# Four PSUM banks in two shared pairs, one run of value products, fp16 projection halves in a macaron block

## The chip, the cores and the metric

The kernel runs on one core of one Trainium2 chip. The metric is the device time of one execution in microseconds (us), as the median of several executions. The profile shown is that of one further execution of the same program.

## The reference, cut to what matters

The input has 8 sequences of 1024 rows of 256 channels. Three residual steps follow each other: half a feed-forward step, an attention step, half a feed-forward step with the same weights. All matrices are fp32.

```python
x = x + 0.5 * ffn(layernorm(x))      # r = sigmoid(xr @ Wr.T); out = r * (relu(xk @ Wk.T)**2 @ Wv.T)
x = x + attn(layernorm(x))
x = x + 0.5 * ffn(layernorm(x))
# attn, 16 heads of 16 channels: 40 fixed offsets o (0..32, 48, 64, 96, 128, 192, 256, 384)
lg[i] = (q . k[n - o_i]) / 4 * (1 + q . scale_embed[i]) + pos_bias[i]     # masked where n < o_i
p = softmax over the 40 offsets
out = (sum_i p[i] * v[n - o_i]) * if_gain;  return (out * sigmoid(x @ gate_w.T + gate_b)) @ out_w.T + out_b
```

## The kernel before, in words

Rows are worked on in 32 chunks of 256 (feed-forward and projections) and 64 tiles of 128 (attention). Five Python generators emit the work: `stage_f1` and `stage_f2` (the two feed-forward steps), `stage_p` (projections), `stage_qk` (scores) and `stage_att` (the rest of attention). They are advanced step by step in an order that the constants `TRACE` set, each step under a priority that `RANK` sets. A scheduler then chooses the order of the instructions on each engine from these priorities and its own durations, so an edit at one place moves instructions at many others. [...]

The projections (`stage_p`, `proj`) split both operands in two parts, `xh`, `xl` and `wa_hi`, `wa_lo`, and add three products (high·high, high·low, low·high). The parts are of type fp32r, a rounded fp32 of four bytes. There are 4 projections of 12 products in each chunk, so 1536 products of 128 rows x 128 columns x 256.

The scores (`scores`, called by `stage_qk`) are products of 32 rows of queries with keys, four of them side by side in the columns of the array: 16 or 32 of them fill one PSUM tile `p`. ScalarE copies it out (line 308). The results go to HBM (`sl_d` for the near offsets, `sf_d` for the far ones) and come back skewed, as `lg` and `ef`.

For each tile, `stage_att` forms the position products `gp` (two halves of 8 products), and VectorE multiplies them into `lg` (lines 405 and 410). GpSimd adds the bias, VectorE takes the maximum and subtracts it, ScalarE takes the exponential. The probabilities of the near offsets go to HBM and come back as `pd` (lines 426 and 428), in one single buffer. TensorE transposes `pd` in two groups of four (`tra`, line 464), ScalarE copies each group out as `ptt` (line 470), and 32 small value products fill `pv`. VectorE normalises (lines 481 to 485), TensorE transposes `acc` (line 490), VectorE gates it into `yt` (line 491), and for each second tile the output projection follows and is added to `x1` (line 505).

PSUM has eight banks, and before the change each holds one tag with one buffer: `psa`, `psb` and `psp` for the chunks, `psq` for scores, `gp`, `pst` for the transposes of `pd`, `pv`, and `psy` for the transposes of `acc` and for the output projection. A tile can be written only when its tag's buffer has been read out:

```python
p = ps.tile([128, 512], F32, name="p", tag="psq")          # scores
gp = ps.tile([128, 64, 8], F32, name="gp")                 # position products
tr = ps.tile([128, 512], F32, name="tra", tag="pst")       # transposes of pd
tr = ps.tile([128, 512], F32, name="tra", tag="psy")       # transposes of acc, output projection
```

Of the kernel before, what the change touches and what calls it, by code (L numbers as in the profile page):

```python
# [7 lines left out]

F32 = mybir.dt.float32
F32R = mybir.dt.float32r  # L10
F16 = mybir.dt.float16
I32 = mybir.dt.int32
AF = mybir.ActivationFunctionType
ALU = mybir.AluOpType
# [11 lines left out]
NL = LW + 1  # L26
# [11 lines left out]
VPAD = 96  # L38
VROW = 2 * 8 * 17
F2A = 28  # L40
TRACE = (0, 3.6, -4.4, -8.1, -10.6)
RANK = (0, 5.1, -4.4, -8.1, -10.6)

# [6 lines left out]
def macaron(ctx: ExitStack, tc: tile.TileContext, x, wffn, watt, wo, cols, rows, pbias, se, mask, out):  # L50
    nc = tc.nc
    pool = lambda name, bufs, **k: ctx.enter_context(tc.tile_pool(name=name, bufs=bufs, **k))
    const = pool("const", 1)
# [7 lines left out]
    mu_r, mu_k, b_q, b_k, b_g, gain, slot = (col[:, 2 * i : 2 * i + 2] for i in range(7))  # L61
    wot = const.tile([128, 2, 256], F32, name="wot")
    row = const.tile([128, 2, 256], F32, name="row")
    bv, bo = row[:, 0], row[:, 1]
    bias = const.tile([128, NO * 16], F32, name="bias")
    msk = const.tile([128, 3, NO], F32, name="msk")
    wa_hi = const.tile([128, 4, 2, 256], F32R, name="wa_hi")
    wa_lo = const.tile([128, 4, 2, 256], F32R, name="wa_lo")
    seb = const.tile([128, 2, NO], F16, name="seb")
    half = const.tile([128, 4], F32, name="half")  # L70
    nc.gpsimd.memset(half, -0.5)
# [10 lines left out]
    pw = pool("pw", 1)  # L82
# [10 lines left out]
    def load_att():  # L93
        with tc.tile_pool(name="setup", bufs=1) as sp:
            wst = sp.tile([128, 4, 2, 256], F32, name="wst")
            nc.sync.dma_start(wst, watt.rearrange("w (c p) d -> p w c d", p=128))
            nc.vector.tensor_scalar(wst[:, 0], wst[:, 0], 0.25, None, ALU.mult)
            nc.vector.tensor_copy(wa_hi, wst)
            nc.vector.tensor_tensor(wa_lo, wst, wa_hi.bitcast(F32), ALU.subtract)
            nc.vector.tensor_scalar(b_q, b_q, 0.25, None, ALU.mult)  # L100
            nc.vector.tensor_scalar(b_g, b_g, 0.5, None, ALU.mult)
            nc.sync.dma_start(row, rows.unsqueeze(0).to_broadcast([128, 2, 256]))
            for t in [t.bitcast(F32) for t in kb] + vw:
                nc.gpsimd.memset(t, 0.0)
            zero = kb[1].bitcast(F32).rearrange("p a b w -> p (a b w)")
            for i in range(2):
                nc.sync.dma_start(v_d[i][0 : VPAD * VROW].rearrange("(p w) -> p w", p=VPAD), zero[:VPAD, :VROW])
            nc.sync.dma_start(sf_d[0:PADF].rearrange("(p w) -> p w", p=16), zero[:16, : PADF // 16])
            for c0, c1, w in ((0, 8, 384), (8, 15, 384), (15, 16, 368)):
                o = PADF + c0 * ROW + ROW - 384  # L110
                nc.sync.dma_start(flat(sf_d, o, (SF_T, 32), (ROW, c1 - c0), (1, w)), zero[:32, : (c1 - c0) * w])
            nc.sync.dma_start(flat(pd_d, NL * 16, (4 * SKEW, 128), (SKEW, 4), (1, SKEW - NL * 16)), zero[:, : 4 * 512])
            nc.sync.dma_start(bias, pbias.to_broadcast([128, NO * 16]))
            nc.sync.dma_start(msk, mask.rearrange("t p u -> p t u"))
            nc.sync.dma_start(wot, wo.rearrange("(c p) d -> p c d", p=128))
            for c in range(2):
                nc.vector.tensor_scalar(wot[:, c], wot[:, c], gain[:, c : c + 1], 0.5, ALU.mult, ALU.mult)
            se_f = sp.tile([128, NO], F32, name="se_f")
            se_h = sp.tile([128, NO], F16, name="se_h")
            for h2 in range(2):  # L120
                nc.sync.dma_start(se_f[64 * h2 : 64 * h2 + 64], se.unsqueeze(1).to_broadcast([16, 4, NO]))
            nc.vector.memset(seb, 0.0)
            nc.vector.tensor_scalar(se_f, se_f, 4.0, None, ALU.mult)
            nc.vector.tensor_copy(se_h, se_f)
            nc.vector.tensor_tensor(se_f, se_f, se_h, ALU.subtract)
            nc.vector.tensor_scalar(se_f, se_f, slot[:, 1:2], None, ALU.mult)
            for h2 in range(2):
                a = slice(64 * h2, 64 * h2 + 64)
                nc.vector.scalar_tensor_tensor(seb[a, h2], se_h[a], slot[a, 0:1], se_f[a], ALU.mult, ALU.add)
# [3 lines left out]
    def mm(o, l, r, start, stop):  # L133
        nc.tensor.matmul(o, l, r, start=start, stop=stop)  # L134
# [98 lines left out]
    def stage_p():  # L233
        for c in range(NCH):
# [4 lines left out]
            gt = gate[c] = pga.tile([128, 2, 256], F32, name="gt")  # L239
            s = "b" if c == 1 else "p"  # L240
            tr = norm_transposed(x1[c], y, nb, 2 * k, s)
            xh = pw.tile([128, 2, 256], F32R, name="xh", tag="xk" + s)
            xl = pw.tile([128, 2, 256], F32R, name="xl", tag="xr" + s)
            nc.scalar.copy(xh, tr)
            nc.vector.tensor_tensor(xl, tr, xh.bitcast(F32), ALU.subtract)

            def proj(w):
                p = ps.tile([128, 2, 256], F32, name="p", tag="ps" + s)
# [21 lines left out]
                        nc.sync.dma_start(flat(qk_d[i % 2][j], o + ro, (2048, 128), (s2, 2), (1, 256)), hl)  # L270
            p = proj(3)
            for g in range(2):
                nc.scalar.activation(gt[:, g], p[:, g], AF.Tanh, bias=b_g[:, g : g + 1], scale=0.5)
            p = ps.tile([128, 512], F32, name="p", tag="ps" + s)
            for k in range(2):
                first = True
# [20 lines left out]
    def stage_qk():  # L297
        def scores(o, g, q4, q, k, keys):

            p = ps.tile([128, 512], F32, name="p", tag="psq")  # L300
            for pr in range(4):
                for s in range(len(q4(0))):
                    for a in range(4):
                        pp = p[32 * a : 32 * a + 32, pr * 128 : pr * 128 + 128].rearrange("n (h j) -> n h j", h=2)
                        w = 64 // len(q4(a))
                        ms = q4(a)[s]
                        mm(pp[:, :, s * w : s * w + w], q[:, pr, ms], k[:, pr, :, keys(ms)], True, True)
            nc.scalar.copy(o[:, :, :, g], p.rearrange("n (q h j) -> n j h q", q=4, h=2))  # L308

        for i in range(2 * B):  # L310
            hf = i % 2
# [57 lines left out]
    def stage_att():  # L369
        for tt in range(B * NT):  # L370
# [25 lines left out]
                v3[:, 2].rearrange("p h w -> p (h w)"), flat(v_d[b % 2], o - 48 * VROW, (VROW, 128), (1, VROW))  # L396
            )
            for h2 in range(2):
                gp = ps.tile([128, 64, 8], F32, name="gp")
                for g in range(2):  # L400
                    for pr in range(4):
                        q = qs[i, g][:, pr, t4 * 128 : t4 * 128 + 128]
                        mm(gp[:, 0:NO, 4 * g + pr], q, seb[:, h2], True, True)
                e = slice(8 * h2, 8 * h2 + 8)
                nc.vector.scalar_tensor_tensor(
                    lg[:, 0:NL, e], gp[:, 0:NL], 1.0, lg[:, 0:NL, e], ALU.add, ALU.mult
                )
                for k0, k1 in FARG:
                    w0, w1 = (24 - FAR[k] // 16 for k in (k0, k1 - 1))
                    nc.vector.scalar_tensor_tensor(  # L410
                        lf[:, k0:k1, e],
                        gp[:, NL + k0 : NL + k1],
                        1.0,
                        ef[:, w0 : w1 + 1 : (w1 - w0) // (k1 - k0 - 1), e],
                        ALU.add,
                        ALU.mult,
                    )
# [39 lines left out]
                nc.vector.tensor_tensor(o, terms[:, 0:m], terms[:, n - m : n], ALU.add)  # L457
                n -= m

            pv = ps.tile([128, 2, 8, 17], F32, name="pv")  # L460
            for g in range(2):
                tr = ps.tile([128, 512], F32, name="tra", tag="pst")
                for pr in range(4):
                    nc.tensor.transpose(  # L464
                        tr[:, pr * 128 : pr * 128 + 128],
                        pd.rearrange("p (m e) -> p m e", e=8)[:, :, 4 * g + pr],
                        ident,
                    )
                ptt = pw.tile([128, 4, 128], F32, name="ptt")
                nc.scalar.copy(ptt.rearrange("p q n -> p (q n)"), tr)  # L470
                for pr in range(4):
                    for q in range(4):
                        mm(
                            pv[32 * q : 32 * q + 32, :, 4 * g + pr],
                            ptt[:, pr, q:128:4],
                            vwt[:, q, :, 4 * g + pr],
                            True,
                            True,
                        )
            rc = pstat.tile([128, 16], F32, name="rc")  # L480
            nc.vector.tensor_tensor(rc, pv[:, :, :, 16:17].rearrange("p a b o -> p (a b o)"), fs, ALU.add)
            nc.vector.reciprocal(rc, rc)
# [2 lines left out]
            nc.vector.tensor_tensor(a16(acc), a16(acc), rc.unsqueeze(2).to_broadcast([128, 16, 16]), ALU.mult)  # L485
            if n0 == 0:
                yt = pw.tile([128, 2, 256], F32, name="yt")
            tr = ps.tile([128, 512], F32, name="tra", tag="psy")
            for h in range(2):
                nc.tensor.transpose(tr[:, h * 128 : h * 128 + 128], acc[:, h * 128 : h * 128 + 128], ident)  # L490
            nc.vector.scalar_tensor_tensor(
# [5 lines left out]
                ALU.mult,  # L497
            )
            if n0:
                p = ps.tile([128, 512], F32, name="tra", tag="psy")  # L500
                for k in range(2):
                    for h in range(2):
                        mm(p[:, k * 256 : k * 256 + 256], yt[:, h, k * 128 : k * 128 + 128], wot[:, h], h == 0, h == 1)
                xx = x1[c].rearrange("p t c -> p (t c)")
                nc.vector.tensor_tensor(xx, xx, p, ALU.add)
# [80 lines left out]
```

## Time and profile before

| | |
|---|---|
| median of 3 runs | 1262.62 us (1255.21 to 1265.52) |
| the profiled execution, its own time | 1256.76 us |
| its span, first to last instruction | 1254.0 us |
| mean granted TensorE clock | 0.956 |
| TensorE matmul busy | 1089.2 us (87%) |
| VectorE busy | 942.6 us (75%) |
| GpSimd busy | 766.5 us (61%) |
| ScalarE busy | 538.0 us (43%) |
| DMA | 282.88 MB, mean 226 GB/s |

PE stands for TensorE's matmuls, PEld for its weight loads, DVE for VectorE, ACT for ScalarE, POOL for GpSimd, SP for the engine that issues most DMAs; SPq and PEq are their sequencers. A matmul's duration is its latency, and matmuls overlap; what one costs is read from the distance of the starts in the timeline. An fp32 product stands in the profile as two records. A line of the waits names the waiting engine and line, then what ended the wait, then the total in us, the number of waits and the longest.

### The profile page before, as it was taken

To read this page: it belongs to the slowest core of one execution; us is meant where nothing else is said; L and a number is where in the kernel's file an instruction comes from. 1 tells how busy PE (TensorE), PEld (TensorE's weight loads), DVE (VectorE), ACT (ScalarE), POOL (GpSimd) and SP (SyncE) were. 2 spreads that over 40 slices of the span, in tenths; PEclk is the share of its full clock that TensorE was granted. 3 is DMA by queue.
4 is the path that set the end of the run, shared out by engine and by line. 5 is a ranking of instruction groups with operands and counts; after the bars stand their busy time and mean duration, and the time that the engine had idled before them with its cause. 6 is when DMAs were issued, how large, how long until landed. Compare 5 with 4: busy or idle time off the path is not lost.

```text
span 1254.0 us, 34712 instructions
## 1 busy us (share of the span) xinstructions
PE 1089.2 (87%) x13568; PEld 885.7 (71%) x13568; DVE 942.6 (75%) x2266; ACT 538.0 (43%) x1025; POOL 766.5 (61%) x1101
## 2 busy tenths in 40 slices
PE   2887989899799898989899989899988998888785
PEld 2676768677687677777777778786777787665664
DVE  7546768987587888879678866978858887877772
ACT  2444445344453444536345454544534444524231
POOL 7436619675575656659457564867656755657672
PEclk9999999899999999899999999999989999998988
DMA  8187888786878779787788977797787868998630
GB/s 263 32 224 222 241 242 265 229 238 194 251 226 254 230 233 274 221 252 232 193 260 257 254 201 230 228 269 227 233 243 234 269 197 254 284 280 265 202 99 24
DMA packets 256500, 282.88 MB, mean 226 GB/s; under 512 B 23440, under 2 KB 214608, under 8 KB 256336
## 3 DMA queue, kind: packets, MB, share of 16 engines
q1 hardware_dynamic: 247120, 263.36, 71.7%
q10 hardware_dynamic: 9216, 17.31, 3.8%
q8 instruction: 106, 1.74, 0.6%
q14 instruction: 58, 0.48, 0.1%
HBM read 151.67 MB, written 128.91 MB: 224 GB/s over the span
## 4 chain that ended last, share of the span: by engine, by line
PE 42%; DMA 25%; DVE 14%; SPq 6%; POOL 5%; issue 5%; ACT 4%; POOLq 0%; ACTq 0%; DVEq 0%
PE p L134 29%; DMA pd<-pd 9%; PE tra L464 4%; PE pv L134 3%; PE tra L134 3%; POOL prod L445 2%; DMA lg<-sl 2%; DMA x<-in_x_dram 2%; DMA qk<-hl 2%; DMA kb<-qk 2%; DMA sl<-sl 2%; DVE prod L457 2%; DVE xk L196 1%; PE gp L134 1%; DVE mx L423 1%
## 5 line engine op out<-in xcount | busy, mean ns | idle before, releaser
L134 PEld LDWEIGHTS <-qst 128*32 128x32 f16 (+1 forms) x5120 | 157.2, 120 | 100.1 <-issue 63.5
L134 PE MATMUL p<-kb,qst 128*32 128x128 f16 (+1 forms) x4096 | 185.1, 297 | 12.7 <-ACT sl L308 8.6
L308 ACT COPY sl<-p 128x512 f32<-128x512 f32 x224 | 130.8, 584 | 144.2 <-PE p L134 123.0
L445 POOL TENSOR_TENSOR prod<-v,lg 128x256 f32<-128x256 f32 x248 | 165.5, 687 | 10.2 <-ACT lg L425 6.1
L134 PE MATMUL p<-xk,w_f 128*128 128x256 f32 x512 | 144.9, 421 | 20.0 <-DVE xk L196 11.7
L419 POOL TENSOR_TENSOR lg<-lg,bias 128x640 f32<-128x640 f32 x64 | 113.5, 1774 | 71.8 <-DVE lg L410 66.9
L213 POOL TENSOR_TENSOR x<-x,xr 128x512 f32<-128x512 f32 x64 | 88.4, 1382 | 109.0 <-DVE xr L212 94.9
L457 DVE TENSOR_TENSOR prod<-prod 128x512 f32<-128x512 f32 (+2 forms) x120 | 126.1, 1051 | 32.1 <-POOL prod L445 31.5
L464 PE MATMUL tra<-ident,pd 128*128 128x128 f32 x512 | 97.1, 313 | 58.3 <-DMA pd<-pd 54.9
L160 ACT ACTIVATE xn<-x,nb,y 128x256 f32<-128x256 f32 x192 | 110.8, 602 | 63.0 <-DVE nb L152 55.2
L134 PE MATMUL p<-w_f,xk 128*128 128x256 f32 x512 | 132.9, 400 | 1.7 <-ACT xr L206 1.3
L134 PE MATMUL p<-w_f,xr 128*128 128x256 f32 x512 | 130.4, 396 | 3.6 <-ACT xk L201 2.8
L445 POOL TENSOR_TENSOR prod<-vn,lg 128x256 f32<-128x256 f32 x144 | 96.0, 678 | 54.3 <-ACT lg L425 35.4
L134 PE MATMUL p<-xh,wa_hi 128*128 128x256 f32 x384 | 123.2, 321 | 5.6 <-DVE hl L264 4.4
L134 PEld LDWEIGHTS p<-xk,w_f 128*128 128x128 f32 x512 | 99.3, 208 | 39.8 <-issue 10.5
L470 ACT COPY ptt<-tra 128x512 f32<-128x512 f32 x128 | 74.9, 585 | 116.1 <-PE tra L464 113.0
L464 PEld LDWEIGHTS tra<-ident,pd 128*128 128x128 f32 x512 | 71.0, 197 | 73.9 <-DMA pd<-pd 68.0
L263 ACT ACTIVATE hl<-p,col 128x256 f16<-128x256 f32 x128 | 60.6, 474 | 121.1 <-PE p L134 68.6
L134 PE MATMUL p<-xh,wa_lo 128*128 128x256 f32 x384 | 111.5, 290 | 0.0
L134 PE MATMUL p<-xl,wa_hi 128*128 128x256 f32 x384 | 111.4, 290 | 0.0
L134 PEld LDWEIGHTS p<-w_f,xr 128*128 128x128 f32 x512 | 95.3, 196 | 19.4 <-ACT xk L201 5.8
L134 PEld LDWEIGHTS p<-w_f,xk 128*128 128x128 f32 x512 | 96.0, 198 | 15.9 <-issue 2.8
(82 smaller groups left out, 2394.2 us busy)
## 6 DMA issues: line engine op xcount, KB each, us to landing
qk<-hl SPq DMA_DIRECT2D x256, 128.0 KB, 3.4
sl<-sl SPq DMA_DIRECT2D x256, 128.0 KB, 3.8
pd<-pd SPq DMA_DIRECT2D x64, 512.0 KB, 4.8
sf<-sl SPq DMA_DIRECT2D x184, 128.0 KB, 3.1
vw<-vd SPq DMA_DIRECT2D x128, 136.0 KB, 4.1
v<-vd SPq DMA_DIRECT2D x64, 272.0 KB, 4.3
lg<-sl SPq DMA_DIRECT2D x64, 264.0 KB, 4.1
pd<-lg ACTq DMA_DIRECT2D x64, 264.0 KB, 3.8
```

What stands on the lines that cost most here:

```text
L134: nc.tensor.matmul(o, l, r, start=start, stop=stop)
L160: nc.scalar.activation(xn, x2[:, i], AF.Identity, bias=nb[:, k : k + 1], scale=y[:, k : k + 1])
L196: nc.vector.scalar_tensor_tensor(o[:, h], xr[:, h], mu[:, h : h + 1], prev[:, h], ALU.mult, ALU.add)
L213: nc.gpsimd.tensor_tensor(x2, x2, xr, ALU.add)
L263: nc.scalar.activation(hl[:, 0], p[:, g], AF.Identity, bias=bb[:, g : g + 1])
L308: nc.scalar.copy(o[:, :, :, g], p.rearrange("n (q h j) -> n j h q", q=4, h=2))
L419: nc.gpsimd.tensor_tensor(la, la, bias, ALU.add)
L423: nc.vector.tensor_reduce(mx, lg.rearrange("p u e -> p e u"), AX.X, ALU.max)
L445: nc.gpsimd.tensor_tensor(prod[:, k], shifted[k][1]()[:, :, 0:16], lf[:, k].unsqueeze(2).to_broadcast([128, 16, 16]), ALU.mult,)
L457: nc.vector.tensor_tensor(o, terms[:, 0:m], terms[:, n - m : n], ALU.add)
L464: nc.tensor.transpose(tr[:, pr * 128 : pr * 128 + 128], pd.rearrange("p (m e) -> p m e", e=8)[:, :, 4 * g + pr], ident,)
L470: nc.scalar.copy(ptt.rearrange("p q n -> p (q n)"), tr)
```

## The change

It has three parts. First, four of the eight PSUM banks are shared in pairs: scores and `gp` have the tag `psq` with two buffers, and the transposes of `pd`, the transposes of `acc` and the output projection have the tag `pst` with two buffers. Second, both copies of the transposed `pd` go into one `ptt` of double size, and the 32 value products of a tile stand together after them, from head group 7 down to 0. The first waits for the second copy, and the others are emitted to follow it. Third, the projection halves become fp16; the weights are scaled by `WS` = 16, and the scale is taken out again where the results are read. For that, the copy of the scores gets a factor, two more small scalings and one longer one stand in the setup, and the rounding of `wa_hi` moves from VectorE to ScalarE.

```diff
-    wa_hi = const.tile([128, 4, 2, 256], F32R, name="wa_hi")
-    wa_lo = const.tile([128, 4, 2, 256], F32R, name="wa_lo")
+    wa_hi = const.tile([128, 4, 2, 256], F16, name="wa_hi")
+    wa_lo = const.tile([128, 4, 2, 256], F16, name="wa_lo")
...
-            nc.vector.tensor_scalar(wst[:, 0], wst[:, 0], 0.25, None, ALU.mult)
-            nc.vector.tensor_copy(wa_hi, wst)
-            nc.vector.tensor_tensor(wa_lo, wst, wa_hi.bitcast(F32), ALU.subtract)
+            nc.vector.tensor_scalar(wst[:, 0], wst[:, 0], 0.25 * WS, None, ALU.mult)
+            nc.vector.tensor_scalar(wst[:, 1:4], wst[:, 1:4], WS, None, ALU.mult)
+            nc.scalar.copy(wa_hi, wst)
+            nc.vector.tensor_tensor(wa_lo, wst, wa_hi, ALU.subtract)
...
-            xh = pw.tile([128, 2, 256], F32R, name="xh", tag="xk" + s)
-            xl = pw.tile([128, 2, 256], F32R, name="xl", tag="xr" + s)
+            xh = pw.tile([128, 2, 256], F16, name="xh", tag="xh" + s)
+            xl = pw.tile([128, 2, 256], F16, name="xl", tag="xl" + s)
...
-            p = ps.tile([128, 512], F32, name="p", tag="psq")
+            p = ps.tile([128, 512], F32, name="p", tag="psq", bufs=2)
...
-            nc.scalar.copy(o[:, :, :, g], p.rearrange("n (q h j) -> n j h q", q=4, h=2))
+            nc.scalar.mul(o[:, :, :, g], p.rearrange("n (q h j) -> n j h q", q=4, h=2), WS**-3)
...
-                gp = ps.tile([128, 64, 8], F32, name="gp")
+                gp = ps.tile([128, 64, 8], F32, name="gp", tag="psq", bufs=2)
...
-            pv = ps.tile([128, 2, 8, 17], F32, name="pv")
+            ptt = pw.tile([128, 8, 128], F32, name="ptt")
             for g in range(2):
-                tr = ps.tile([128, 512], F32, name="tra", tag="pst")
+                tr = ps.tile([128, 512], F32, name="tra", tag="pst", bufs=2)
...
-                ptt = pw.tile([128, 4, 128], F32, name="ptt")
-                nc.scalar.copy(ptt.rearrange("p q n -> p (q n)"), tr)
-                for pr in range(4):
-                    for q in range(4):
-                        mm(
-                            pv[32 * q : 32 * q + 32, :, 4 * g + pr],
-                            ptt[:, pr, q:128:4],
-                            vwt[:, q, :, 4 * g + pr],
-                            True,
-                            True,
-                        )
+                nc.scalar.copy(ptt[:, 4 * g : 4 * g + 4].rearrange("p q n -> p (q n)"), tr)
+
+            pv = ps.tile([128, 2, 8, 17], F32, name="pv")
+
+            def values(ms):
+                return [
+                    nc.tensor.matmul(
+                        pv[32 * q : 32 * q + 32, :, m], ptt[:, m, q:128:4], vwt[:, q, :, m], start=True, stop=True
+                    )
+                    for m in ms
+                    for q in range(4)
+                ]
+
+            first = values((7,))[0]
+            with tc.issue_after(first.ins):
+                values((6, 5, 4, 3, 2, 1, 0))
...
-            tr = ps.tile([128, 512], F32, name="tra", tag="psy")
+            tr = ps.tile([128, 512], F32, name="tra", tag="pst", bufs=2)
...
-                p = ps.tile([128, 512], F32, name="tra", tag="psy")
+                p = ps.tile([128, 512], F32, name="tra", tag="pst", bufs=2)
```

More of the change, by code (lines that the diff above doesn't have):

```diff
@@ L9 @@
 F32 = mybir.dt.float32
-F32R = mybir.dt.float32r
 F16 = mybir.dt.float16
@@ L40 @@
 F2A = 28
+WS = 16.0
 TRACE = (0, 3.6, -4.4, -8.1, -10.6)
@@ L96, in load_att @@
             nc.sync.dma_start(wst, watt.rearrange("w (c p) d -> p w c d", p=128))
-            nc.vector.tensor_scalar(wst[:, 0], wst[:, 0], 0.25, None, ALU.mult)
-            nc.vector.tensor_copy(wa_hi, wst)
-            nc.vector.tensor_tensor(wa_lo, wst, wa_hi.bitcast(F32), ALU.subtract)
-            nc.vector.tensor_scalar(b_q, b_q, 0.25, None, ALU.mult)
+            nc.vector.tensor_scalar(wst[:, 0], wst[:, 0], 0.25 * WS, None, ALU.mult)
+            nc.vector.tensor_scalar(wst[:, 1:4], wst[:, 1:4], WS, None, ALU.mult)
+            nc.scalar.copy(wa_hi, wst)
+            nc.vector.tensor_tensor(wa_lo, wst, wa_hi, ALU.subtract)
+            nc.vector.tensor_scalar(b_q, b_q, 0.25 * WS, None, ALU.mult)
+            nc.vector.tensor_scalar(b_k, b_k, WS, None, ALU.mult)
             nc.vector.tensor_scalar(b_g, b_g, 0.5, None, ALU.mult)
             nc.sync.dma_start(row, rows.unsqueeze(0).to_broadcast([128, 2, 256]))
+            nc.vector.tensor_scalar(bv, bv, WS, None, ALU.mult)
             for t in [t.bitcast(F32) for t in kb] + vw:
@@ L116, in load_att @@
             for c in range(2):
-                nc.vector.tensor_scalar(wot[:, c], wot[:, c], gain[:, c : c + 1], 0.5, ALU.mult, ALU.mult)
+                nc.vector.tensor_scalar(wot[:, c], wot[:, c], gain[:, c : c + 1], 0.5 / WS, ALU.mult, ALU.mult)
             se_f = sp.tile([128, NO], F32, name="se_f")
@@ L241, in stage_p @@
             tr = norm_transposed(x1[c], y, nb, 2 * k, s)
-            xh = pw.tile([128, 2, 256], F32R, name="xh", tag="xk" + s)
-            xl = pw.tile([128, 2, 256], F32R, name="xl", tag="xr" + s)
+            xh = pw.tile([128, 2, 256], F16, name="xh", tag="xh" + s)
+            xl = pw.tile([128, 2, 256], F16, name="xl", tag="xl" + s)
             nc.scalar.copy(xh, tr)
-            nc.vector.tensor_tensor(xl, tr, xh.bitcast(F32), ALU.subtract)
+            nc.vector.tensor_tensor(xl, tr, xh, ALU.subtract)
             def proj(w):
@@ L272, in stage_p @@
             for g in range(2):
-                nc.scalar.activation(gt[:, g], p[:, g], AF.Tanh, bias=b_g[:, g : g + 1], scale=0.5)
+                nc.scalar.activation(gt[:, g], p[:, g], AF.Tanh, bias=b_g[:, g : g + 1], scale=0.5 / WS)
             p = ps.tile([128, 512], F32, name="p", tag="ps" + s)
@@ L405, in stage_att @@
                 nc.vector.scalar_tensor_tensor(
-                    lg[:, 0:NL, e], gp[:, 0:NL], 1.0, lg[:, 0:NL, e], ALU.add, ALU.mult
+                    lg[:, 0:NL, e], gp[:, 0:NL], WS, lg[:, 0:NL, e], ALU.add, ALU.mult
                 )
@@ L412, in stage_att @@
                         gp[:, NL + k0 : NL + k1],
-                        1.0,
+                        WS,
                         ef[:, w0 : w1 + 1 : (w1 - w0) // (k1 - k0 - 1), e],
```

## The prediction

> **What bounds the kernel now.** I read the engine rows first, then the chain that ended last, then the waits, and last the timeline of the middle, instruction by instruction.
>
> ```profile
> PE 1089.2 (87%) x13568; PEld 885.7 (71%) x13568; DVE 942.6 (75%) x2266; ACT 538.0 (43%) x1025; POOL 766.5 (61%) x1101
> ...
> PE 42%; DMA 25%; DVE 14%; SPq 6%; POOL 5%; issue 5%; ACT 4%; POOLq 0%; ACTq 0%; DVEq 0%
> ```
>
> TensorE is the busiest engine, and the chain runs through it for 42% of the span, not for all of it. A quarter of the chain is DMA. So TensorE is the first bound but not a wall: time saved on it comes back as something between its share of the chain and the whole.
>
> ```profile
> PEld tra L464 <- DMA pd<-pd: 68.0, 38, 7.3
> PE tra L464 <- DMA pd<-pd: 54.9, 33, 7.2
> DVE lg L405 <- DMA lg<-sl: 33.6, 18, 6.1
> PE gp L134 <- DVE lg L410: 10.1, 9, 2.4
> PE p L134 <- ACT sl L308: 8.6, 9, 4.4
> ```
>
> TensorE's largest idle time is at the transposes of `pd`, when its round trip through HBM is late: 54.9 us (the PEld row tells the same time for the loads). The two waits for single banks, `gp` behind its eviction and scores behind their copy, are only 10.1 and 8.6 us. VectorE stands still for 33.6 us in front of an `lg` that has not landed; that row matters below.
>
> ```profile
> SPq L428 <- PE tra L464: 13.4, 4, 9.7
> ...
> SPq L428 <- PE p L134: 8.6, 12, 1.7
> ```
>
> Line 428 issues the read of `pd`. Its one buffer is free only when both groups of the tile before are transposed, and SP waits for that (22.0 us in these two rows).
>
> ```profile
> 607.35 0.39 PE L134 MATMUL p<-xh,wa_hi 128*128 128x256 f32 x1
> 607.57 0.28 PE L134 MATMUL p<-xl,wa_hi 128*128 128x256 f32 x1
> 607.69 0.28 PE L134 MATMUL p<-xh,wa_lo 128*128 128x256 f32 x1
> ...
> 608.75 0.28 PE L134 MATMUL p<-xh,wa_lo 128*128 128x256 f32 x1
> 608.87 0.50 PE L464 MATMUL tra<-ident,pd 128*128 128x128 f32 x3
> 609.21 0.34 PE L134 MATMUL gp<-seb,qst 128*128 128x40 f16 x5
> 609.48 0.35 PE L134 MATMUL p<-kb,qst 128*32 128x128 f16 x11
> 609.76 0.44 PE L490 MATMUL tra<-ident,acc 128*128 128x128 f32 x2
> 610.13 0.28 PE L134 MATMUL p<-kb,qst 128*32 128x128 f16 x5
> 610.34 0.66 PE L162 MATMUL tr<-ident,xn 128*128 128x128 f32 x4
> ```
>
> Here the price of TensorE's work is seen in the distance of the starts. A projection of 12 products takes 608.87 - 607.35 = 1.52 us: 0.22 us to the second start, then about 0.12 us each. And a change between products over 128 columns of the array and over 32 (scores, values) costs extra: 11 near scores start within 0.13 us (16 of them within 0.19 in the timeline), but the transposes come after 0.28; two transposes at 0.11 are 0.22, but the next scores come after 0.37; 5 scores are 0.06, but 0.21 pass. That is 0.15 us for each change.
>
> **16-bit halves: -22 us of TensorE time.** The count stays at 1536 products with 1536 loads. The trace shows no 256-column fp16 product. From above: no gain, if the 0.12 us stay. From below: an fp32 product's two records of 256 columns start 0.216 us apart, each 2 x 0.108, so a single pass can take 0.108; 12 of them are 1.30 us instead of 1.52, and 128 projections give 28 us. The start of a projection stays partly open, since the load of 128 fp16 columns has a row of 105 ns (`gp`) against 197 ns for fp32r; I take 0.17 us for each, 22 us. The Trainium skill ("TensorE: Matmul & The Clock Gate", Back-to-back issue gap) puts 256 columns at N/2.4 + 2.5 = 109 ns at full clock, an estimate of 114 ns at the granted 0.956; by that the 11 steady distances save 8 us and not 17. I keep the row, since it was taken at this clock. Either way a four-byte type gains little here: it already streams in one pass.
>
> **Runs: -20 us of TensorE time.** I counted the order of the instructions in both built programs. Changes between wide and narrow products fall from 676 to 544; runs of values from 169 to 67, of `gp` from 156 to 119. 132 x 0.15 = 20 us. Values now start behind the second copy (0.585 us, ACT row of `ptt`) and not behind the first; the scheduler has put other work there.
>
> Together -42 us of 1089. By the chain's share, 42 x 0.42 = 18 us reach the end; at most 42. I take 28, because TensorE is idle for only 165 us of the span and the first 60 and the last 54 us hold 44 of these.
>
> **Two banks: -18 us.** The bank waits of 10.1 and 8.6 us can go at most; I take 10, since part of it becomes another wait of the same place. Both groups of transposes no longer share one bank, and 28 runs of eight stand in the new order where before the second group waited for a copy; so `pd` is free earlier and SP's 22.0 us shrink. I take 8, with 0 and 22 as ends. A rule of the skill speaks against the part: the same page (Part 1, HAM oscillation) reports of a kernel with waits for DMA that "Adding PSUM double-buffering gave no further gain". By the rule this part is 0, by the rows 18.
>
> **What sharing costs: +18 us.** Scores now stand behind `gp` in the same two banks, in 116 places of the new order, with 4.3 us of TensorE work between them in the median and under 3 us in 35. The eviction of a half takes 0.42 + 3 x 0.16 = 0.9 us, so it is normally covered. It isn't where VectorE waits for `lg`: then the scores, and behind them everything on TensorE, wait too. At the lower end 0, at the upper all 33.6 us; I take 8. The second group of transposes now waits for the `yt` of the tile before (0.41 us, with 3.3 us of TensorE work in between, 60 places): 4. The order also leaves less TensorE work between the last `gp` of a tile and its first transpose, 16.5 instead of 18.9 us in the median, so the late `pd` is waited for longer: from 0 to 35 stalled tiles x 2.4 = 84 us; half of the 2.4 is only TensorE being faster and counted already, and the scheduler has the chain of `gp` closer together, so I take 6.
>
> **Rest: +2 us.** At the start VectorE's list from 10.93 us to the first `nb` (16.77 us) has `wa_lo` in it, now behind 1.2 us more scaling and a copy of 2048 elements on ScalarE (an estimate of 1.9 us from 0.74 us for 640 elements, 0.58 for 512). The first `xn` comes some 1.6 us later, with nothing over it. The factor in the copy of scores makes it like the other ScalarE reads of PSUM (0.595 against 0.584 us), 224 x 0.011 = 2.5 us on an engine that is 43% busy: hidden. The copies into `xh` and `xl` read fp32 from PSUM as before (0.58 and 0.68 us). The DMAs are the same in number and size.
>
> Sum: -28 - 18 + 18 + 2 = **-26 us**. 1256.76 - 26 = 1231 for the profiled execution; the median of the runs is 0.5% above that execution, which makes **1236**.
>
> **Rivals.**
> *A, the forecast*: TensorE's saving comes through by two thirds, bank gains and losses cancel. 1236, chance 0.42.
> *B, no change*: the round trips of `pd` and `lg` and VectorE's 75% set the pace; the 42 us turn into longer waits at line 464. For it: 25% DMA in the chain, and 16.5 us instead of 18.9. Against it: TensorE is idle for so little. Only a few us are left, 1258; chance 0.15.
> *C, slower*: scores queue behind a `gp` that can't be evicted because its `lg` hasn't landed. Before, a first half kept its bank for 5.7 us in the median and over 13.0 in a quarter of the tiles, the second half for 2.1 and 3.8 (first `gp` product to last VectorE read, tile by tile in the timeline). It decides from the point where the hold passes the 4.3 us of cover. If the new halves behave like the old second ones, nearly nothing shows; if like the old first ones, half the tiles pass it: 16 by about 9 us and 16 by about 1.5 us, which is 168 us. A third of that, less 26, gives +30: 1292. For it: one late `lg` stops VectorE and TensorE together. Against it: both halves now stand closely together and later. Chance 0.25.
> *D, faster yet*: all 42 us come through, both bank waits and SP's 22 us go, and no new wait appears: 1256.76 - 42 - 19 - 22 + 2 = 1176, in the median 1181. All of it at once is too much; I place it around 1200, chance 0.18.
>
> **How the numbers follow.** A and D lie below 1250, the bound of 1% (about what a measurement of this kernel can tell from no change): together 0.60. Within 1%: B, 0.15. Slower: C, 0.25. The range leaves out the far ends of C and D: 1196 to 1284. The forecast's own range, with its ends of -18 and -42 for TensorE, is 1222 to 1247.
>
> **What would show it.** Right: TensorE's rows with `xh` and `xl` near 0.108 us apart and a projection near 1.35 us; TensorE busy near 1045 us; the waits for `sl` L308 and for `lg` L410 in front of TensorE small; 32 value products together. Wrong: projections that still take 1.5 us (first step), TensorE's wait for `pd` well over 55 us (B), or a new large row of scores or loads that wait for VectorE's `lg` (C). A TensorE saving that is there while the span doesn't move would refute the two thirds.

## The result, and the profile after

The changed kernel takes **1296.0 us** (1294.8 to 1303.4) beside 1263.1 us for the kernel before: a ratio of **1.029**, interval 1.024 to 1.034. It is slower; 1236 us and a range up to 1284 us were forecast. Its profiled execution has a span of 1292.8 us.

The engine row and the chain of the changed kernel, from its page:

```profile
PE 1067.8 (83%) x13568; PEld 833.8 (64%) x13568; DVE 939.6 (73%) x2268; ACT 540.8 (42%) x1026; POOL 757.5 (59%) x1101
...
PE 33%; DVE 24%; DMA 24%; POOL 6%; SPq 5%; issue 4%; ACT 3%; POOLq 0%; ACTq 0%; DVEq 0%
```

TensorE is busy for 21.4 us less, and the kernel is 33 us longer. No engine's busy time grew by more than 3 us. So the loss is idle time. In the chain TensorE fell from 42% to 33% and VectorE rose from 14% to 24%: the end waits less for TensorE and more for VectorE.

The waits of the changed kernel (engine and line, what ended the wait, total us, number, longest):

```profile
PE p L138 <- DMA kb<-qk: 43.8, 19, 4.9
PE tra L468 <- DMA pd<-pd: 38.0, 26, 3.5
...
PE tra L499 <- DVE acc L494: 24.9, 18, 4.9
...
PE gp L138 <- ACT sl L312: 7.6, 7, 4.6
PE p L138 <- DVE lg L414: 6.3, 6, 2.1
```

The new row is the first: 43.8 us in which scores wait for a block of keys to arrive (`kb`). Before, it was this:

```profile
PE p L134 <- DMA kb<-qk: 1.6, 1, 1.6
```

TensorE now comes to the scores before their keys do. The row for `pd` is smaller than before (54.9 us). VectorE's wait for `lg`, 33.6 us before, doesn't appear any more; its wait for `gp` has grown instead, before and after:

```profile
DVE lg L405 <- PE gp L134: 20.7, 18, 2.9
```

```profile
DVE lg L409 <- PE gp L138: 35.0, 28, 6.0
```

Where is the time along the span? Two views show it. First the tile view of `gp` (products; min/median/max in ns; first and last start; form), before and after:

```profile
L134 PE MATMUL gp<-seb,qst x1024: 196/207/290, 69.0 to 1192.4; 128*128 128x40 f16 x171
```

```profile
L138 PE MATMUL gp<-seb,qst x1024: 196/207/274, 135.6 to 1211.8; 128*128 128x40 f16 x171
```

The first position product starts at 135.6 us and not at 69.0 us. That is not yet how late attention is: before, the first products lay in their bank until `lg` had landed. The lines of the same view for VectorE's first read of each half, before and after, show when attention goes on:

```profile
L405 DVE SCALAR_TENSOR_TENSOR lg<-gp,lg x128: 363/423/439, 102.7 to 1192.8; 128x264 f32<-128x264 f32 x128
```

```profile
L409 DVE SCALAR_TENSOR_TENSOR lg<-gp,lg x128: 366/424/439, 136.1 to 1221.3; 128x264 f32<-128x264 f32 x128
```

Attention starts 33 us later. Tile by tile this read comes 19 to 54 us later than before, 34 in the median: the lag is there from the first tile, and it is carried to the end. From the tile view of the scores, their last product starts at 1171 us before and at 1177 us after: the scores have lost 6 us. The rest is lost behind them. From the last score to the end of the span 83 us pass before and 116 us after. The windows view from 1150 us to beyond the end shows what is left for the tail (window, length, busy time of PE, PEld, DVE, ACT and POOL with the numbers of instructions, clock, DMA share, GB/s), again before and after:

```profile
1150.00:1310.00 160.00, 76.43 (x782) 58.23 (x778) 63.45 (x150) 28.01 (x50) 54.24 (x76) 0.91 0.27 83
```

```profile
1150.00:1310.00 160.00, 98.21 (x1170) 77.96 (x1168) 93.07 (x217) 39.70 (x70) 78.21 (x108) 0.84 0.40 121
```

At 1150 us VectorE still has 217 instructions in front of it and not 150, and TensorE 1170 and not 782. The scores go nearly at their old pace; the attention of the tiles trails some 34 us further behind them, and at the end there is less left to put beside it.

Why TensorE brings `gp` late is in no wait row, since the order of TensorE's instructions was fixed when the program was built. The trace shows them run in that order: it has 676 changes between wide and narrow products before and 544 after, as the built programs do. For each tile I took from the trace how long `lg`, which VectorE multiplies with `gp`, had been there: from its landing to the tile's first `gp` product 1.7 us pass before and **21.9 us** after (medians over the tiles). The products are ready and stand in the list behind scores. The timeline of the changed kernel shows such scores, which wait themselves:

```profile
405.38 1.17 PE L138 MATMUL p<-kb,qst 128*32 128x128 f16 x16 [1.18 <-DMA kb<-qk]
407.98 1.16 PE L138 MATMUL p<-kb,qst 128*32 128x128 f16 x16 [1.43 <-DMA kb<-qk]
```

The number in brackets is TensorE's idle time ahead of the products. The `lg` of two tiles had landed by then, at 399.7 and 401.1 us, and their `gp` run only at 419.1 and 440.2 us. So the list makes ready work wait for work that is not ready.

The order tells why. The buffers of one tag are handed out in the order in which the program emits the tiles. With scores and `gp` in one tag, a `gp` can take its bank only after all score groups emitted ahead of it have had theirs. I counted, in the built orders of TensorE's instructions, the score groups that are emitted ahead of a `gp` and run behind it: 8.0 in the mean before (124 of the 128 `gp` halves overtake some), **0 after**. The scores are emitted some four tiles ahead of the attention (`TRACE`, last lines of the kernel), and the scheduler had pulled each `gp` forward past eight of their groups. The shared tag forbids that.

### The profile page after: what moved, and what is told of

Same layout as the page of the kernel before. It is cut to its first block, busy times and chain, and to the rows that moved or that the text cites. A ratio compares the mean times of both kernels' runs of the same rounds, so it can differ in the third digit from the quotient of the medians.

```text
span 1292.8 us, 34757 instructions
## 1 busy us (share of the span) xinstructions
PE 1067.8 (83%) x13568; PEld 833.8 (64%) x13568; DVE 939.6 (73%) x2268; ACT 540.8 (42%) x1026; POOL 757.5 (59%) x1101
## 4 chain that ended last, share of the span: by engine, by line
PE 33%; DVE 24%; DMA 24%; POOL 6%; SPq 5%; issue 4%; ACT 3%; POOLq 0%; ACTq 0%; DVEq 0%
PE p L138 24%; DMA kb<-qk 7%; DMA pd<-pd 4%; DVE prod L461 3%; POOL prod L449 3%; DMA x<-in_x_dram 3%; DVE xk L200 2%; DMA qk<-hl 2%; DVE xr L197 2%; PE tra L468 2%; DMA pd<-lg 2%; PE pv L479 2%; DVE xr L200 2%; DVE st L146 2%; PE tra L138 2%
## 5 line engine op out<-in xcount | busy, mean ns | idle before, releaser
L138 PE MATMUL p<-kb,qst 128*32 128x128 f16 (+1 forms) x4096 | 184.1, 298 | 56.5 <-DMA kb<-qk 43.8
L312 ACT ACTIVATE sl<-p 128x512 f32<-128x512 f32 x224 | 130.8, 598 | 133.7 <-PE p L138 104.2
L138 PE MATMUL p<-xk,w_f 128*128 128x256 f32 x512 | 141.6, 416 | 19.4 <-DVE xk L200 14.2
L461 DVE TENSOR_TENSOR prod<-prod 128x512 f32<-128x512 f32 (+2 forms) x120 | 134.9, 1124 | 30.3 <-POOL prod L449 28.1
L217 POOL TENSOR_TENSOR x<-x,xr 128x512 f32<-128x512 f32 x64 | 86.5, 1352 | 103.7 <-DVE xr L216 98.3
L423 POOL TENSOR_TENSOR lg<-lg,bias 128x640 f32<-128x640 f32 x64 | 107.8, 1685 | 54.4 <-DVE lg L414 46.1
L449 POOL TENSOR_TENSOR prod<-vn,lg 128x256 f32<-128x256 f32 x144 | 92.9, 656 | 76.8 <-ACT lg L429 59.7
L138 PE MATMUL p<-xh,wa_hi 128*128 128x256 f16 x384 | 109.0, 284 | 14.5 <-DVE hl L268 9.0
L468 PE MATMUL tra<-ident,pd 128*128 128x128 f32 x512 | 85.1, 301 | 42.4 <-DMA pd<-pd 38.0
L138 PEld LDWEIGHTS p<-w_f,xk 128*128 128x128 f32 x512 | 97.7, 201 | 23.5 <-issue 5.1
L138 PE MATMUL p<-xl,wa_hi 128*128 128x256 f16 x384 | 108.6, 283 | 0.0
L138 PE MATMUL p<-xh,wa_lo 128*128 128x256 f16 x384 | 108.2, 282 | 0.0
```

Source lines behind the costliest of these rows:

```text
L217: nc.gpsimd.tensor_tensor(x2, x2, xr, ALU.add)
L312: nc.scalar.mul(o[:, :, :, g], p.rearrange("n (q h j) -> n j h q", q=4, h=2), WS**-3)
L423: nc.gpsimd.tensor_tensor(la, la, bias, ALU.add)
L449: nc.gpsimd.tensor_tensor(prod[:, k], shifted[k][1]()[:, :, 0:16], lf[:, k].unsqueeze(2).to_broadcast([128, 16, 16]), ALU.mult,)
L468: nc.tensor.transpose(tr[:, pr * 128 : pr * 128 + 128], pd.rearrange("p (m e) -> p m e", e=8)[:, :, 4 * g + pr], ident,)
```

## The experiments

**Theory, the order of the shared banks:** scores and `gp` in one tag force `gp`, and with it everything that follows in a tile, behind the scores emitted ahead of it; the time is lost because attention trails. **Rival:** the sharing is harmless, and the loss comes from elsewhere in the change: the fp16 halves or the new order around them, `pd` or `acc`, or banks that are held too long.

### The shared tag alone, and everything but it

`own_banks` is the changed kernel with scores and `gp` in a bank each, as before; `psq_only` is the kernel before with that one sharing.

```diff
# own_banks, against the kernel after
-p = ps.tile([128, 512], F32, name="p", tag="psq", bufs=2)
+p = ps.tile([128, 512], F32, name="p", tag="psq")
-gp = ps.tile([128, 64, 8], F32, name="gp", tag="psq", bufs=2)
+gp = ps.tile([128, 64, 8], F32, name="gp")
# psq_only, against the kernel before
-p = ps.tile([128, 512], F32, name="p", tag="psq")
+p = ps.tile([128, 512], F32, name="p", tag="psq", bufs=2)
-gp = ps.tile([128, 64, 8], F32, name="gp")
+gp = ps.tile([128, 64, 8], F32, name="gp", tag="psq", bufs=2)
```

> The changed kernel, but scores and position products have one bank of their own each again; the transposes still share two, the value products still stand in one run, the halves are still fp16. Theory 'order of the shared banks': the two buffers are handed out in the order in which the program emits the tiles, so every gp waits for all scores emitted before it (on average 8 score groups that ran after it before now run ahead of it); attention runs later and the end with it. It expects 1225 to 1250 us here, with the last gp near 1180 us and the lag of gp behind the scores as before. Rival 'transposes': sharing the two transpose banks makes TensorE wait for acc and yt; it expects 1280 to 1300 us here, since that sharing is still in. Rival 'fp16 shifts the schedule': also 1280 to 1300 us.

> The kernel before, with only the sharing of two banks by scores and position products. Theory 'order of the shared banks': the whole loss is here, 1290 to 1310 us, last gp 15 to 25 us later than before with the last score at nearly the same time. Rival 'transposes' and rival 'fp16 shifts the schedule': 1245 to 1265 us.

Measured: `own_banks` 1257.1 us, ratio **0.996** (0.994 to 0.998); `psq_only` 1302.6 us, ratio **1.031** (1.028 to 1.035). The sharing of scores and `gp` by itself costs all that the change costs, and the change without it costs nothing. The tile view of `gp`, first of `psq_only`, then of `own_banks`:

```profile
L134 PE MATMUL gp<-seb,qst x1024: 196/207/274, 134.7 to 1231.1; 128*128 128x40 f16 x171
```

```profile
L138 PE MATMUL gp<-seb,qst x1024: 196/207/274, 69.2 to 1175.5; 128*128 128x40 f16 x171
```

The start moves with the tag; VectorE's first read comes at 135.1 us in `psq_only` and at 103.7 in `own_banks`. So does the count of overtaken score groups: 0 in `psq_only`, 7.8 in `own_banks`; and the distance from `lg` to `gp`: 23.5 us, and in `own_banks` -2.5 us (in more than half of the tiles the first products start before `lg` has landed). Three numbers that the theory expected were off. `own_banks` came out above its range of 1225 to 1250 us, so the rest of the change brings little. In `psq_only` the last `gp` is 39 us later than before and not 15 to 25, and the last score did not stay where it was, it starts 23 us later (1193.4 us). A wait row of `own_banks` shows the price that the sharing was meant to remove:

```profile
PE gp L138 <- DVE lg L414: 30.1, 20, 4.0
```

30.1 us of waiting for the one `gp` bank, and yet it is faster by 39 us than the changed kernel, where this row has 1.5 us.

### The fp16 halves alone

`f16_only` is the kernel before with the fp16 halves and their scales; banks and values stay.

```diff
-xh = pw.tile([128, 2, 256], F32R, name="xh", tag="xk" + s)
-xl = pw.tile([128, 2, 256], F32R, name="xl", tag="xr" + s)
+xh = pw.tile([128, 2, 256], F16, name="xh", tag="xh" + s)
+xl = pw.tile([128, 2, 256], F16, name="xl", tag="xl" + s)
# and wa_hi, wa_lo in F16 with the factors WS of the change
```

> The kernel before, with only the fp16 halves and their scaling. Theory 'order of the shared banks': 1235 to 1260 us, since a projection is some 0.2 us shorter and nothing else moves. Rival 'fp16 shifts the schedule': 1280 us or more.

Measured: 1266.7 us, ratio **1.001** (0.999 to 1.003). The engine row and the first wait row of this kernel:

```profile
PE 1071.6 (85%) x13568; PEld 842.9 (67%) x13568; DVE 927.9 (73%) x2268; ACT 547.3 (43%) x1026; POOL 761.4 (60%) x1101
```

```profile
PE tra L468 <- DMA pd<-pd: 83.5, 34, 5.4
```

TensorE's busy time falls by 17.6 us, and its wait for `pd` rises from 54.9 to 83.5 us. The time lies between the ranges of the two theories. TensorE's work is less, and a longer wait at the same transposes stands against it. Neither the loss nor a gain comes from here.

### The same buffers, emitted in another order

If the order of emission is what hurts, it can be mended without touching a bank. The first number of `TRACE` sets how many tiles earlier the steps of attention are emitted; `RANK`, their priority, stays.

```diff
# att_earlier, against the kernel after
-TRACE = (0, 3.6, -4.4, -8.1, -10.6)
+TRACE = (-2, 3.6, -4.4, -8.1, -10.6)
# att_one_earlier: -1 in the same place
# psq_att_earlier: psq_only with -2
```

> The changed kernel, with the attention steps emitted two steps earlier (first number of TRACE -2 in place of 0), so that fewer scores stand ahead of each gp in the order of the shared banks. Theory 'order of the shared banks': the lag of gp falls by about 6 score groups, and the time by more than half of the loss: 1250 to 1275 us. Rivals 'transposes' and 'fp16': no change beyond the noise of a new schedule, 1285 to 1305 us.

> The kernel before with only the sharing of two banks by scores and position products, and the attention steps emitted two steps earlier. Theory 'order of the shared banks': the loss of the sharing alone goes away, 1240 to 1265 us against 1303 without the earlier emission, and the last gp is again within 20 us of the last score. Rival 'two users in two banks': scores stand behind the eviction of gp wherever they are emitted, and the time stays over 1285 us; the gain of the earlier emission in the whole change would then need fp16 or the shared transposes.

> The changed kernel with the attention steps emitted one step earlier in place of two. Theory 'order of the shared banks': the time follows the number of score groups ahead of a gp, so it lies between the changed kernel (1296) and the one with two steps (1243), about 1260 to 1280 us. Rival 'luck of one schedule': no order, anything from 1240 to 1300 us, outside that middle.

Measured:

| kernel | ratio (interval) | score groups run before the first `gp` | from `lg` to `gp`, us |
|---|---|---|---|
| after | 1.029 (1.024 to 1.034) | 16 | 21.9 |
| att_one_earlier | 1.015 (1.012 to 1.018) | 12 | 17.5 |
| att_earlier | **0.984** (0.978 to 0.990) | 8 | 5.9 |
| psq_only | 1.031 (1.028 to 1.035) | 16 | 23.5 |
| psq_att_earlier | **0.986** (0.982 to 0.990) | 8 | 6.0 |

The same instructions in the same banks go from 1296 us to **1242.8 us**, and one tile lies between none and two. `att_earlier` beats both kernels, and by more than the theory's range (1250 to 1275 us) allowed; the other two fall into theirs. The kernel before, with a bank each, was not run with the earlier emission. So how much of the 1.5% that these kernels gain over it belongs to the earlier emission by itself is not known. The tile view of its `gp` and the windows view of its tail:

```profile
L138 PE MATMUL gp<-seb,qst x1024: 196/207/274, 94.7 to 1169.3; 128*128 128x40 f16 x171
```

```profile
1150.00:1310.00 160.00, 62.76 (x690) 49.05 (x690) 57.37 (x132) 23.39 (x41) 46.44 (x67) 0.91 0.20 60
```

At 1150 us VectorE has 132 instructions left, fewer than the 150 of the kernel before. And its wait rows, of the same kind as above:

```profile
PE p L138 <- DVE lg L414: 17.1, 15, 2.9
PE p L138 <- DMA kb<-qk: 13.5, 5, 4.9
...
PE tra L468 <- DMA pd<-pd: 10.4, 6, 4.3
```

The wait for keys falls from 43.8 to 13.5 us, the wait for `pd` from 38.0 to 10.4 us. Holding the banks (17.1 us at `p` behind the last read of `gp`) has become more frequent than in the slow kernel: it is there, and it is small.

The granted clock doesn't decide it: it is 0.956 before, 0.935 after and 0.945 in `att_earlier`, but 0.934 in `own_banks`, which is as fast as the kernel before.

### Pairs made differently

`scores_two_own` keeps two buffers for scores, gives `gp` a bank of its own and pays for it with a single bank for all transposes and the output projection.

```diff
# against the kernel after
-gp = ps.tile([128, 64, 8], F32, name="gp", tag="psq", bufs=2)
+gp = ps.tile([128, 64, 8], F32, name="gp")
-tr = ps.tile([128, 512], F32, name="tra", tag="pst", bufs=2)
+tr = ps.tile([128, 512], F32, name="tra", tag="pst")
# the same at the two other tiles of tag pst
```

> The changed kernel with two banks for the scores alone, one for gp alone, and one single bank for all transposes and the output projection. Theory 'order of the shared banks': gp is free again, so no loss of 3%: 1245 to 1270 us, with some waits of TensorE for yt and acc in front of the one transpose bank. Rival 'two score banks let the scores run ahead of attention': the loss stays, 1280 us or more.

Measured: 1382.7 us, ratio **1.098** (1.094 to 1.102). The theory missed its range. The rival's "1280 us or more" covers the number but not by its reason: the scores did not keep their pace while attention fell behind, since the last score is 92 us later than before and the last `gp` 108 us. `gp` is free of the order here (7.3 groups overtaken), so the theory's own mechanism is gone, and something else costs 9.8%. One wait row stands out, with 14.3 us and 8 times in the kernel before:

```profile
POOL prod L449 <- DVE acc L461: 119.7, 51, 8.2
```

GpSimd's products of one tile wait for VectorE's sums of the tile before. I read this as the tiles going one after the other: in one tag, in order of emission, the transposes of `pd` of a tile stand behind the output projection of the tile before, and this behind its whole normalisation. That is argued from the order; no run tells it from other causes.

### The second buffer of `pd`

The wait that swallowed the gain of fp16 is for `pd`, whose single buffer delays the read. With fp16 halves a second one fits into SBUF.

```diff
# f16_two_pd, against f16_only
-pd = pat.tile([128, ROW], F32, name="pd", bufs=1)
+pd = pat.tile([128, ROW], F32, name="pd", bufs=2)
# att_earlier_two_pd: the same edit on att_earlier
# f16_psq_two_pd: f16_two_pd with scores and gp in one tag and TRACE at -2
```

> The kernel before with the fp16 halves and a second buffer for pd. Theory 'late pd takes the saving': with fp16 alone TensorE saved 18 us of busy time and waited 28.6 us longer for pd; if the single pd buffer makes pd late, the wait falls below 50 us here and the time to 1235 to 1255 us. Rival 'the round trip itself is late': the wait stays near 80 us and the time near 1265 us.

> The changed kernel with the attention steps emitted two steps earlier and a second buffer for pd. If the two remedies add up, 1215 to 1235 us (1243 with the first alone, 1237 for fp16 with the second alone). Rival 'the transposes that stand together have freed pd early already': no further gain, 1238 to 1250 us.

> The kernel before with fp16 halves, the sharing of two banks by scores and position products, attention emitted two steps earlier and a second buffer for pd; transposes, output projection and value products as before. If the shared transposes and the value run are worth something, it is slower than the kernel of the same call that has them, by 5 to 15 us; if not, the same or faster, 1215 to 1235 us.

Measured: `f16_two_pd` 1237.3 us, ratio **0.985** (0.980 to 0.989); `att_earlier_two_pd` 0.987 (0.983 to 0.991); `f16_psq_two_pd` 0.990 (0.987 to 0.993). The first kernel gets a gain where `f16_only` had none. TensorE's wait for `pd` in it is

```profile
PE tra L468 <- DMA pd<-pd: 47.5, 28, 6.0
```

where `f16_only` has 83.5 us. SP's waits for the buffer in front of the read, 14.4 and 4.3 us in `f16_only` (the two rows that the prediction read), are gone. But on top of the earlier emission the second buffer brings nothing more, and the three remedies together are no better than one. Nor is the shared pair of transposes with the run of values shown to be worth anything in time: `f16_psq_two_pd`, which lacks both, takes 1254.1 us and `att_earlier_two_pd` 1250.6, and their intervals overlap. In `att_earlier` the row of `pd` had only 10.4 us left, which is one reason; in `f16_psq_two_pd` 27.8 us of it are back. What holds all three at about 0.985 stays open. The second buffer without fp16 wasn't tried; so its share in the 1.6% that `f16_two_pd` gains over `f16_only` includes what fp16 brings once it is released.

## Why the prediction was wrong, step by step

**16-bit halves: right in size.** From the timeline of the changed kernel:

```profile
602.27 0.27 PE L138 MATMUL p<-xh,wa_hi 128*128 128x256 f16 x1
602.38 0.27 PE L138 MATMUL p<-xl,wa_hi 128*128 128x256 f16 x1
602.49 0.27 PE L138 MATMUL p<-xh,wa_lo 128*128 128x256 f16 x1
...
603.47 0.27 PE L138 MATMUL p<-xh,wa_lo 128*128 128x256 f16 x1
603.58 0.60 PE L138 MATMUL p<-w_f,xk 128*128 128x256 f32 x2
```

The starts are 0.109 us apart (forecast 0.108), a projection takes 603.58 - 602.27 = 1.31 us (forecast 1.35). TensorE's busy time in `f16_only` falls by 17.6 us of the forecast 22 (the next part weighs this with the clock). Over all 1397 recorded distances within projections the median is 109 ns and the mean 117 (before 120 and 135). Row and rule don't differ here, as it turns out: the clock was granted in full at both places of the timeline that were used (granted clock 1.00 in these windows), and the 0.114 us came from scaling the rule by the mean of the whole span. The section that the rule comes from (the Trainium skill, "TensorE: Matmul & The Clock Gate", Back-to-back issue gap) gives N/2.4 + 2.5 for an isolated product and says that a stream of loads and products departs from it; here the stream meets it.

**Runs, and the share that reaches the end: the second was wrong.** TensorE's busy time fell by 21.4 us in all and not by 42 (1067.8, forecast 1045). Much of the difference is the clock. Where the trace has a granted clock of 0.5, the records of the feed-forward products start 427 ns apart, and 216 where it has 1.0; there are 110 us at 0.5 before, 154 in `f16_only` and 168 after. Busy time weighted moment by moment with this clock (taken as full in the first 25 us, where the trace has none), an estimate of the work, is 1041 us before, 1011 in `f16_only` and 999 after: 42 us less, as forecast, with more from fp16 (30, forecast 22) and less from the rest (12, forecast 20). But the two thirds of the saving that were to reach the end don't reach it. `f16_only` gains nothing in time, and its wait for `pd` is 28.6 us longer; `own_banks`, the change without the sharing of scores and `gp`, gains 0.4%, about 5 us, where the prediction took 28 from TensorE alone. For this step rival B described what happens.

**Two banks: the waits moved.** Of the two rows of 10.1 and 8.6 us, 1.5 and 4.6 us are left, but in their place stand 7.6 us (`gp` behind the copy of scores) and 6.3 us (scores behind the last read of `gp`): 18.7 us before, 20.0 after. SP's two rows for `pd`, 22.0 us, became 17.5 us (forecast -8), while its wait at the same line for the write of `pd` to land rose from 17.8 to 46.5 us. What the prediction weighed as a rule is the report of one kernel, in which double-buffered PSUM brought no further gain (the Trainium skill, "TensorE: Matmul & The Clock Gate", Part 1, HAM oscillation). It came nearer than the rows: in the changed kernel the part is worth 5 us at SP at most, and nothing at the banks.

**What sharing costs, +18 us: the step that failed.** It asked how long each bank is held and whether the work in between covers it. That cost is there and small: the 6.3 us above instead of 8. It did not ask in what order the shared buffers are handed out, and so put that cost at nothing. For the sharing of scores and `gp` the prediction had 10 us of gain at the banks against 8 of cost; `psq_only` puts the whole of it at +3.1%, about 40 us, with its gains already in. Of the 59 us between the forecast change (-26) and the measured one (+33), some 40 are this step, and most of the rest is the TensorE saving that did not come through. The term of the transposes was low as well: the wait of the `acc` transposes rose from 9.0 to 24.9 us, with 4 forecast for `yt` (0.6 us); how much of it is the sharing was not separated, and `own_banks`, which has it too (16.5 us), is not slower than before. The term of `pd` (+6 us) had the wrong sign in the wait row of the whole change, 38.0 us after 54.9; in `psq_only`, with the sharing alone, the row did rise, to 74.7 us.

The sign of this could have been had before any run. The built order was at hand, and the prediction counted changes and runs in it; the start of the first `gp`, behind 16 score groups instead of none, was in the same lists.

**Rest, +2 us: right.** The first `xn` comes at 18.00 us and not at 16.95, 1.05 us later (forecast 1.6); what that adds at the end was not measured. The copy of scores takes 598 ns (forecast 595), hidden.

**The rivals.** The time is near C's 1292 us by luck, not for C's reason. C had scores and VectorE stopped by a late `lg`; VectorE's 33.6 us of waiting for it are gone, since the first `gp` of a tile now comes 21.9 us after it in the median. "A large row of scores that wait for VectorE's `lg`", named as its sign, has 6.3 us.

## What to carry to other kernels

Before two kinds of tiles share a tag, look at the order in which they are emitted, not only at how long each holds a buffer: the tag ties the two streams together in that order, and a scheduler can't take one past the other any more. Count in the built order what one stream had been overtaking; if it isn't zero, change the emission with the sharing (here two tiles earlier made 1.029 into 0.984). And a saving on the busiest engine is worth what the next wait leaves of it: with fp16 halves alone 17.6 us of busy time became nothing, and with a second `pd` buffer beside them the kernel gained 1.5%.

## What the runs showed of the hardware

- A load of 128 fp16 columns for the projections takes 98 ns and the fp32r load 188 ns (medians), but the distance of the products falls only from 120 to 109 ns. With half the load the stream is a tenth shorter; whether the load makes this tenth wasn't tried.
- Far scores, whose queries and keys are taken at every sixteenth row, are much slower than near ones: 16 of them take 1.17 us from first start to last end in the timeline above (start to start 0.76 us, the median before of the 64 groups with this shape), while 16 near ones start within 0.19 us. Both have the same tile shape and type. Which of the two operands costs this wasn't tried.
